# Seventeen gathered blocks instead of sixteen in the last block of a graph network, and a dense part of eight chunks of 512 nodes

## The chip, the cores and the metric

The kernel runs on one core of a Trainium2 chip. The metric is device time in microseconds: the median of three runs is 6218.43 us (6216.05 to 6231.69). The profiled execution of the same kernel took 7895.7 us, of which the trace covers 7893.8 us, so it is 1677 us longer than the median of the unprofiled runs. The trace does not say which parts of the kernel are shorter without the profiler; that gap matters for everything below.

## The reference: what is computed

A graph of N = 6250 nodes with 128 features each, and E = 106,250 directed edges sorted by destination, goes through four graph networks one after the other, each with a residual sum and a layer norm around it. The last one holds most of the work: three layers of three hops, nine hops in all, each of which sums weighted neighbour rows.

```
deg  = segment_sum(edge_attr, dst);  dinv = rsqrt(deg) where deg > 0, else 0
w    = dinv[src] * edge_attr * dinv[dst]
h    = node
for l in range(3):
    out, x = h @ W[l, 0], h
    for k in range(1, 4):
        x   = segment_sum(w[:, None] * x[src], dst)
        out = out + x @ W[l, k]
    y = h + out + bias[l]
    h = relu(layernorm(y) * gamma[l] + beta[l])
```

The first three networks do the same kind of sum with unweighted edges (a mean, and twice a symmetric normalisation).

## The kernel before

**Tiling.** The 6250 nodes are NW = 49 blocks of P = 128. The blocks of destination nodes are grouped into NC = 13 chunks, whose sizes in blocks are given by RUNS (line 64) and listed in SHAPE; START holds the first block of each. A chunk of four blocks is 512 columns, one of three is 384.

**Two ways to sum over neighbours.** A dense chunk uses an adjacency matrix in DRAM. For the unweighted sums this matrix is `counts` (one byte per cell) for all 13 chunks. For the nine weighted hops it is `weights` (four bytes per cell), made only for the first ND = 9 chunks, that is blocks 0 to 32. Both matrices are zeroed by transfers on SyncE's queue (`empty`) and then filled by GpSimd with scattered writes (`scatter`, line 571): 17 per block of edge rows. The other 16 blocks, GW = 33 to 48 with NG = 16, have no `weights`: in each hop GpSimd gathers their source rows, KG = 19 indirect transfers of 128 rows per block (line 1021, tile `rows`). ScalarE and VectorE multiply each gathered row by its edge weight and split it in two parts (lines 1055 and 1056, tile `both`), and TensorE adds the parts up with a one-hot matrix (line 1059, accumulator `gacc`). The one-hot matrices are made by VectorE (line 1037).

**A dense hop.** For each of the ND chunks TensorE multiplies the 49 blocks of the table of the hop before (`hop`) by 49 slices of `weights`, which arrive two at a time on SyncE's queue (tile `weighed`, line 453 issues, line 1091 multiplies, accumulator `acc`). A matmul of plain float32 shows as two MATMUL rows in the trace, so 441 products per hop are 882 rows.

**Order.** TensorE's order in the nine hops is fixed in the program. The class `Stream` (line 984) keeps a clock of its own, with a cost for each kind of work in its constants: DENSE for a product of 512 columns, GATHERED for a gathered product, SMALL and WIDE for the products at the end of a chunk, PACE for the time between two gathers on GpSimd, LAND for the time until gathered rows are usable. `take` puts a gathered product into TensorE's order when the planned landing time has come; `hop` puts the dense products there. The chip then runs this order as it stands: a gathered product that is not ready holds up every dense product behind it. GpSimd may run ahead by 26 gathers of the 30 row slots. The first gather of a hop waits until every block of the hop before is stored (`store`, line 893); `hop_end` does the closing work of a chunk (lines 925 to 981: transposes L419, small products L427 and L942).

**Ahead of the hops.** A first loop over the 13 chunks builds `counts` on GpSimd (`count_cells`, `cell` on VectorE) while TensorE computes the degrees (line 696) and the first sums (line 492). In the same loop `weights` is zeroed for chunks 0 to ND - 1, and from chunk ND - 1 on the second convolution's sums over the first KNOWN = START[ND] blocks are begun for chunks 0 to 7. Then `weights` is filled while TensorE works through the remaining unweighted sums, and three fetches for each gathered block (line 811) bring in its edges.

Of the kernel before, what the change touches and what calls it, by code (L numbers as in the profile page):

```python
# [33 lines left out]
F32 = mybir.dt.float32  # L34
# [4 lines left out]
I32 = mybir.dt.int32  # L39
# [8 lines left out]
P = 128  # L48
# [12 lines left out]
CW = 512  # L61
WPC = CW // P

RUNS = [(6, 4), (3, 3), (4, 4)]
SHAPE = [n for count, n in RUNS for _ in range(count)]
START = [sum(SHAPE[:c]) for c in range(len(SHAPE))]
NC = len(SHAPE)

KD = 17
# [2 lines left out]
assert KD * N == E and NB == NW  # L72
NEAR = 3

ND = 9
GW = range(START[ND], NW)
NG = len(GW)
PAIRS = [slice(w, min(w + 2, NW)) for w in GW[::2]]
# [6 lines left out]
SLOTS, LOADS, STEP, HOTS, GROUP = 30, 12, 2, 5, 4  # L85
# [17 lines left out]
def width(c):  # L103
    return len(windows_of(c)) * P
# [6 lines left out]
def near(i):  # L111
    begin = min(max(i - 1, 0), NW - NEAR)
    return range(begin, begin + NEAR)
# [6 lines left out]
def chunks_near(i):  # L120
    return sorted({chunk_of(near(i)[0]), chunk_of(near(i)[-1])})
# [53 lines left out]
def kernel(ctx: ExitStack, tc: tile.TileContext, a: dict, out: bass.AP):  # L175
# [13 lines left out]
    counts = dram.tile([BASE[NC], 1], U8, name="counts")  # L189
    weights = dram.tile([BASE[ND], 1], F32, name="weights")  # L190
    zeros = top.tile([P, 7 * CW // 16], F32, name="zeros")
# [162 lines left out]
    with tc.If(go == 1) as fork:  # L354
        usual_way(tc, a, out, dram, ident, part, first, recs, edges, counts, weights, fills, empty)
# [5 lines left out]
def usual_way(ctx, tc, a, out, dram, ident, part, first, recs, edges, counts, weights, fills, empty):  # L361
# [3 lines left out]
    work = ctx.enter_context(tc.tile_pool(name="work", bufs=2))  # L365
# [134 lines left out]
    def evicted(acc, cw, more=None):  # L500

        if more is not None:
            nc.vector.tensor_add(more[:, :cw], acc[:, :cw], more[:, :cw])
            return more
        t = sums_room()
        nc.scalar.copy(t[:, :cw], acc[:, :cw])  # L506
        return t
# [4 lines left out]
    celli = early.tile([P, NB, KD], I32, name="celli")  # L512
    dense = [i for i in range(NB) if chunks_near(i)[0] < ND]
    wval = early.tile([P, len(dense), KD], F32, name="wval")
# [14 lines left out]

    KNOWN, AHEAD = START[ND], 8  # L530
    halves = {c: dram.tile([P, width(c)], F32, name=f"half{c}") for c in range(1, NC)}
# [82 lines left out]
    with tc.tile_pool(name="counted", bufs=2) as counted, tc.tile_pool(name="cells", bufs=1) as cells, \  # L614
# [6 lines left out]
        def beside(x):  # L621

            return bass.AP(x.tensor, x.offset, [*x.ap[:-1], [1, KD], [1, J]])
# [6 lines left out]
        def cell(i, m):  # L630

            c0, c1 = chunks_near(i)[0], chunks_near(i)[-1]
            dst, source = m[:, F_DST:F_DST + KD], m[:, F_CELL:F_CELL + KD]
            mine = m[:, F_KEY + J:F_KEY + J + KD].unsqueeze(2).to_broadcast([P, KD, J])
            same = hots.tile([P, KD, J], BF16, name="same", bufs=1)
            before = hots.tile([P, KD, J], BF16, name="before", bufs=1)
            f1 = work.tile([P, KD], F32, name="f1")
            f2 = work.tile([P, KD], F32, name="f2")
            f3 = work.tile([P, KD], F32, name="f3")
            low = work.tile([P, KD], I32, name="low")  # L640
            dloc = cells.tile([P, KD], F32, name="dloc", bufs=12)
            lw = cells.tile([P, KD, 4], BF16, name="lw", bufs=12)
            degs[i] = dloc, lw
            w = m[:, F_W:F_W + KD]
            nc.vector.tensor_tensor(before[:], beside(m[:, F_KEY:F_KEY + KD]), mine, op=ALU.is_equal)
            nc.vector.tensor_reduce(f3[:], before[:], AX.X, ALU.max)
            nc.vector.tensor_tensor(same[:], beside(m[:, F_KEY + J + 1:F_KEY + J + 1 + KD]), mine, op=ALU.is_equal)
            nc.vector.tensor_reduce(f1[:], same[:], AX.X, ALU.add)
            nc.vector.tensor_scalar_add(cval[:, i, :], f1[:], 1.0)

            nc.vector.scalar_tensor_tensor(f2[:], source, float(width(c0)), dst, op0=ALU.mult, op1=ALU.add)
            nc.vector.tensor_sub(f2[:], f2[:], m[:, F_LOW:F_LOW + KD])
            nc.vector.tensor_scalar_add(f2[:], f2[:], float(BASE[c0] - START[c0] * P))
            if c0 < c1:
                turn, step = START[c1] * P, BASE[c1] - BASE[c0] - (START[c1] - START[c0]) * P
                f4 = work.tile([P, KD], F32, name="f4")
                if width(c0) == width(c1):
                    nc.vector.tensor_scalar(f4[:], dst, float(turn), float(step), op0=ALU.is_ge, op1=ALU.mult)
                else:
                    f5 = work.tile([P, KD], F32, name="f5")  # L660
                    nc.vector.tensor_scalar(f5[:], source, float(width(c1) - width(c0)), float(step),
                                            op0=ALU.mult, op1=ALU.add)
                    nc.vector.scalar_tensor_tensor(f4[:], dst, float(turn), f5[:], op0=ALU.is_ge, op1=ALU.mult)
                nc.vector.tensor_add(f2[:], f2[:], f4[:])
            if (i + 1) * P > ROWS:
                nc.vector.scalar_tensor_tensor(f3[:], dst, float(NOWHERE), f3[:], op0=ALU.is_ge, op1=ALU.add)
            nc.vector.scalar_tensor_tensor(celli[:, i, :], f3[:], FAR, f2[:], op0=ALU.mult, op1=ALU.max)
            nc.vector.tensor_copy(low[:], m[:, F_LOW:F_LOW + KD])
            nc.vector.tensor_tensor(celli[:, i, :], celli[:, i, :], low[:], op=ALU.bitwise_or)
            nc.vector.tensor_scalar_add(dloc[:], dst, -float(near(i)[0] * P))  # L670

            if i in dense:
                ew = hots.tile([P, KD, J], F32, name="ew", bufs=1)
                nc.vector.tensor_tensor(ew[:], same[:], beside(m[:, F_W + 1:F_W + 1 + KD]), op=ALU.mult)
                nc.vector.tensor_reduce(f1[:], ew[:], AX.X, ALU.add)
                nc.vector.tensor_add(wval[:, i, :], w, f1[:])
            nc.vector.tensor_copy(lw[:, :, 0], w)
            nc.vector.tensor_sub(f1[:], w, lw[:, :, 0])
            nc.vector.tensor_copy(lw[:, :, 1], f1[:])
            nc.vector.tensor_sub(lw[:, :, 2], f1[:], lw[:, :, 1])  # L680
            nc.vector.memset(lw[:, :, 3], 1.0)
# [49 lines left out]
        def count_cells(c):  # L731
            for i in fresh(c, counted_blocks):
                cell(i, fetched.pop(i))
                for _ in scatter(counts, U8, cval, i):
                    pass
                counted_blocks.add(i)
# [17 lines left out]
        for c in range(NC):  # L754
# [23 lines left out]
            nc.scalar.dma_start(bases[c][:], x[:])  # L778
            for e in range(2 * (c - ND + 1), 2 * (c - ND + 2)):
                if 0 <= e < AHEAD:  # L780
# [3 lines left out]
                    nc.scalar.dma_start(early_parts[e][:], evicted(acc, width(e), half)[:, :width(e)])  # L784
            if c < ND:
                empty(weights, F32, c, nc.sync)
# [196 lines left out]

    class Stream:

        DENSE, GATHERED, SMALL, WIDE, PACE, LAND, AHEAD = 0.86, 0.12, 0.29, 0.45, 1.26, 7.0, SLOTS - 4

        def __init__(self):
            self.clock = self.pool = 0.0
# [474 lines left out]
```

## Time and profile before

The profile's own time is divided here by the first matmul of line 1091 in each hop.

| What | us |
|---|---|
| Median of the runs | 6218.4 |
| Profiled execution, its span | 7895.7, 7893.8 |
| From the start to the first hop | 3227.2 |
| Nine hops, sum | 4666.6 |
| A hop, six without and three with the layer's end | 505 to 521, 534 |
| TensorE busy in the hops | 3938.6 |
| GpSimd busy in the hops | 2704.2 |
| One gather on GpSimd, median and mean busy time | 0.944, 0.988 |

Engine names in the profile: PE is TensorE, PEld its weight loads, DVE VectorE, ACT ScalarE, POOL GpSimd, SP SyncE; a small q behind a name is the engine's issuing sequencer. A row of the timeline gives start, length, engine, line, operation, output and inputs, how many instructions are merged, and in brackets the idle time before it and what ended it. The length of a matmul overlaps with the next one, so durations of matmuls are read from start to start.

### The profile page before, as it was taken

What the parts mean: (1) busy time and instruction counts of PE and PEld (TensorE: products, weight loads), DVE (VectorE), ACT (ScalarE), POOL (GpSimd) and SP (SyncE); (2) the same over time, 40 slices, a digit from 0 to 9 for tenths busy, and PEclk for the clock granted to TensorE, in tenths of its full rate; (3) what the DMA queues carried; (4) which work ended last, traced back from release to release, by engine and by line L of the source; (5) the groups of instructions that cost most, each with busy time, mean ns of one, the idle gap of its engine ahead of it and who ended that gap; (6) DMA issues with size and microseconds to landing.
All of it is one profiled execution on the core that took longest, in us unless ns stands there. A gap on an engine that the chain in (4) does not pass through costs nothing. (4 is left out here: it accounts for less than half of the span.)

```text
span 7893.8 us, 73018 instructions
## 1 busy us (share of the span) xinstructions
PE 5805.9 (74%) x20184; PEld 3479.6 (44%) x20184; DVE 2979.8 (38%) x8549; ACT 1995.5 (25%) x4437; POOL 4220.2 (53%) x4207
## 2 busy tenths in 40 slices
PE   1354544339668499789798888897888978878887
PEld 0132333117556388445344454453444534434444
DVE  5344323112555256333232452332324423333355
ACT  1122223115344244222121221221212212122122
POOL 5655455640556501364664654646646556466464
PEclk8666767559879799899898998998989989989898
DMA  7444543013343245577677776776767767777776
GB/s 229 125 148 120 168 136 103 13 30 97 106 116 103 56 130 151 194 264 269 229 263 238 256 244 238 276 266 225 260 240 254 248 234 273 244 248 257 253 279 214
DMA packets 720126, 1539.01 MB, mean 195 GB/s; under 512 B 136004, under 2 KB 349144, under 8 KB 719448
## 3 DMA queue, kind: packets, MB, share of 16 engines
q1 hardware_dynamic: 536448, 1292.14, 48.4%
q0 software_dynamic: 134496, 181.90, 7.9%
q10 hardware_dynamic: 48760, 60.19, 2.2%
q8 instruction: 161, 2.64, 0.1%
q14 instruction: 261, 2.14, 0.1%
HBM read 1337.46 MB, written 196.32 MB: 194 GB/s over the span
## 5 line engine op out<-in xcount | busy, mean ns | idle before, releaser
L1091 PE MATMUL acc<-weighed,hop 128*128 128x512 f32 (+1 forms) x7938 | 3681.6, 581 | 336.0 <-issue 326.9
L1021 POOL DMA_INDIRECT rows<-stored,gsrc x2736 | 2704.2, 988 | 2028.4 <-issue 866.7
L1091 PEld LDWEIGHTS acc<-weighed,hop 128*128 128x128 f32 x7938 | 1374.7, 198 | 1423.8 <-issue 1174.2
L1059 PE MATMUL gacc<-both,oh 128*128 128x256 f32 x2736 | 1733.2, 641 | 99.7 <-issue 98.0
L1055 ACT ACTIVATE both<-rows,gwgt 128x128 fp32r<-128x128 f32 x2736 | 879.2, 390 | 2895.0 <-issue 1115.7
L1056 DVE SCALAR_TENSOR_TENSOR both<-rows,gwgt,both 128x128 fp32r<-128x128 f32 x2736 | 831.6, 348 | 1525.2 <-ACT both L1055 718.8
L492 PE MATMUL acc<-wides,t 128*128 128x512 f32 (+1 forms) x3105 | 969.7, 422 | 559.6 <-ACT wides L481 316.3
L571 POOL DMA_INDIRECT counts<-cval,celli x833 | 856.6, 1028 | 591.4 <-issue 248.5
L571 POOL DMA_INDIRECT weights<-wval,celli x578 | 607.3, 1051 | 656.0 <-PE acc L492 479.9
L492 PEld LDWEIGHTS acc<-wides,t 128*128 128x128 f32 x3105 | 617.3, 208 | 752.9 <-ACT wides L481 396.6
L1059 PEld LDWEIGHTS gacc<-both,oh 128*128 128x128 f32 x2736 | 541.0, 198 | 731.1 <-issue 582.5
L1037 DVE TENSOR_TENSOR oh<-iota,gdst 128x640 fp32r<-128x640 f16 x576 | 453.9, 788 | 1030.1 <-remote 356.8
L481 ACT CAST wides<-slots 128x1024 fp32r<-128x1024 uint8 (+3 forms) x687 | 572.2, 863 | 932.2 <-remote 480.1
L492 PE MATMUL acc<-widev,t 128*128 128x512 f32 (+1 forms) x2034 | 594.6, 402 | 62.2 <-DVE widev L481 45.6
L695 DVE TENSOR_SCALAR oh<-iota,dloc 128x384 bf16<-128x384 f16 x833 | 225.8, 324 | 893.5 <-remote 428.6
L492 PEld LDWEIGHTS acc<-widev,t 128*128 128x128 f32 x2034 | 386.3, 198 | 146.0 <-DVE widev L481 66.3
L696 PE MATMUL pd<-oh,lw 128*4 128x384 bf16 x833 | 211.6, 370 | 253.6 <-issue 160.7
L481 ACT CAST wides<-cols 128x1024 fp32r<-128x1024 uint8 (+1 forms) x364 | 286.9, 797 | 402.0 <-PE acc L492 166.4
L481 DVE CAST widev<-cols 128x1024 fp32r<-128x1024 uint8 (+1 forms) x364 | 243.0, 669 | 343.8 <-PE acc L492 208.3
L696 PEld LDWEIGHTS <-lw 128*4 128x4 bf16 x833 | 66.3, 88 | 336.4 <-issue 290.4
L481 DVE CAST widev<-slots 128x1024 fp32r<-128x1024 uint8 (+2 forms) x237 | 155.1, 665 | 121.3 <-remote 53.8
L492 PE MATMUL half<-wides,t 128*128 128x512 f32 (+1 forms) x594 | 186.8, 395 | 0.0
(232 smaller groups left out, 2813.0 us busy)
## 6 DMA issues: line engine op xcount, KB each, us to landing
weighed<-weights SPq DMA_DIRECT2D x1296, 512.0 KB
weighed<-weights SPq DMA_DIRECT2D x648, 384.0 KB
slots<-counts SPq DMA_DIRECT2D x173, 448.0 KB
weights<-zeros SPq DMA_DIRECT2D x6, 12544.0 KB
cols<-counts SPq DMA_DIRECT2D x140, 448.0 KB
rows<-stored,gsrc POOLq DMA_INDIRECT x2736
counts<-zeros SPq DMA_DIRECT2D x10, 3136.0 KB
weights<-zeros SPq DMA_DIRECT2D x3, 9408.0 KB
```

What stands on the lines that cost most here:

```text
L481: copy(wide[:, :n * cw], t[:, r * cw:(r + n) * cw])
L492: product = nc.tensor.matmul(into[:, :cw], lhs, cols, start=s == begin and i == 0, stop=s == end - 1 and i == len(lhss) - 1).ins
L571: ins = nc.gpsimd.indirect_dma_start(out=mat[:], out_offset=bass.IndirectOffsetOnAxis(ap=celli[:, i, k:k + 1], axis=0), in_=vals[:, i, k:k ...
L695: nc.vector.tensor_scalar(oh[:], iota[:], dloc[:, k:k + 1], None, op0=ALU.is_equal)
L696: nc.tensor.matmul(acc[:], lw[:, k, :], oh[:], start=k == 0, stop=k == KD - 1)
L1021: nc.gpsimd.indirect_dma_start(out=fetched_rows[:, self.slot(self.asked), :], out_offset=None, in_=stored[self.h % 2][:], in_offset=bass.I ...
L1037: nc.vector.tensor_tensor(oh[:, :m, :], iota[:, :P].unsqueeze(1).to_broadcast([P, m, P]), gdst[:, i, ks].unsqueeze(2).to_broadcast([P, m, ...
L1055: nc.scalar.activation(both[:, :D], x, AF.Copy, scale=w)
L1056: nc.vector.scalar_tensor_tensor(both[:, D:], x, w, both[:, :D].bitcast(F32), op0=ALU.mult, op1=ALU.subtract)
L1059: nc.tensor.matmul(self.acc[:, j * 2 * D:(j + 1) * 2 * D], self.oh[:, k % HOTS, :], both, start=k == 0, stop=k == KG - 1)
L1091: nc.tensor.matmul(acc[:, :cw], tables[h][:, s, :], t[:, s % STEP * cw:(s % STEP + 1) * cw], start=s == 0, stop=s == NW - 1)
```

## The change

Three constants and four allocations change. RUNS gives ten chunks of four blocks and then three of three, in place of six, three of three, and four. With ND = 8 the weighted dense part is chunks 0 to 7, all of 512 columns (blocks 0 to 32 become 0 to 31), and GW becomes blocks 32 to 48, so NG is 17: eight pairs and a single block at the end. The small tiles f1 to f5 and `low` of `cell` move from the pool `work`, which lives for the whole kernel, to the pool `cells`, which ends with the first loop, with two buffers as before. PACE in the plan goes from 1.26 to 1.2; LAND and the other constants stay.

```diff
-RUNS = [(6, 4), (3, 3), (4, 4)]
+RUNS = [(8, 4), (2, 4), (3, 3)]
...
-ND = 9
+ND = 8
...
-            f1 = work.tile([P, KD], F32, name="f1")
+            f1 = cells.tile([P, KD], F32, name="f1", bufs=2)
...
-            low = work.tile([P, KD], I32, name="low")
+            low = cells.tile([P, KD], I32, name="low", bufs=2)
...
-                f4 = work.tile([P, KD], F32, name="f4")
+                f4 = cells.tile([P, KD], F32, name="f4", bufs=2)
...
-        DENSE, GATHERED, SMALL, WIDE, PACE, LAND, AHEAD = 0.86, 0.12, 0.29, 0.45, 1.26, 7.0, SLOTS - 4
+        DENSE, GATHERED, SMALL, WIDE, PACE, LAND, AHEAD = 0.86, 0.12, 0.29, 0.45, 1.2, 7.0, SLOTS - 4
```

What follows from the constants, without further edits: a hop has 392 dense products of 512 columns where it had 294 of 512 and 147 of 384; it has 323 gathers where it had 304, so 2907 in all for 2736; 200 loads of `weights` per hop for 225; 561 scattered writes into `weights` for 578; 51 fetches of gathered edges for 48; eight zero fills of `weights` for nine; and the early sums of the second convolution begin one chunk earlier and cover 32 blocks for 33, the 33rd being left to the later loop.

More of the change, by code (lines that the diff above doesn't have):

```diff
@@ L636, in cell @@
             before = hots.tile([P, KD, J], BF16, name="before", bufs=1)
-            f1 = work.tile([P, KD], F32, name="f1")
-            f2 = work.tile([P, KD], F32, name="f2")
-            f3 = work.tile([P, KD], F32, name="f3")
-            low = work.tile([P, KD], I32, name="low")
+            f1 = cells.tile([P, KD], F32, name="f1", bufs=2)
+            f2 = cells.tile([P, KD], F32, name="f2", bufs=2)
+            f3 = cells.tile([P, KD], F32, name="f3", bufs=2)
+            low = cells.tile([P, KD], I32, name="low", bufs=2)
             dloc = cells.tile([P, KD], F32, name="dloc", bufs=12)
@@ L659, in cell @@
                 else:
-                    f5 = work.tile([P, KD], F32, name="f5")
+                    f5 = cells.tile([P, KD], F32, name="f5", bufs=2)
                     nc.vector.tensor_scalar(f5[:], source, float(width(c1) - width(c0)), float(step),
```

## The prediction

> **What bounds the kernel now.** I read the page first: PE is busy 74% of the span, POOL 53%, and the slices show two regimes. Up to 3227 us the engines are all half idle; from there on nine hops repeat, 4666.6 us or 59% of the span. The change acts on the hops, so I cut them out by the first matmul of line 1091 and asked for the windows. One typical hop:
>
> ```profile
> core 0: us, PE busy (x) PEld busy (x) DVE busy (x) ACT busy (x) POOL busy (x), PEclk, DMA share, GB/s
> ...
> 5297.80:5805.10 507.30, 433.97 (x1303) 230.51 (x1302) 167.96 (x448) 106.30 (x330) 300.19 (x304) 0.91 0.73 255
> ```
>
> PE is busy 434 of 507 us, POOL 300, DMA 73%: PE is nearest to its limit, but not at it. The busy figure overstates PE, because lengths of matmuls overlap, so I took start-to-start times from PE's timeline where nothing waits:
>
> ```profile
> 5549.81 1.02 PE L1091 MATMUL acc<-weighed,hop 128*128 128x512 f32 x2
> 5550.27 0.68 PE L1059 MATMUL gacc<-both,oh 128*128 128x256 f32 x1
> 5550.79 1.88 PE L1091 MATMUL acc<-weighed,hop 128*128 128x512 f32 x4
> 5552.10 0.68 PE L1059 MATMUL gacc<-both,oh 128*128 128x256 f32 x1
> 5552.62 1.02 PE L1091 MATMUL acc<-weighed,hop 128*128 128x512 f32 x2
> 5553.08 0.68 PE L1059 MATMUL gacc<-both,oh 128*128 128x256 f32 x1
> 5553.59 1.02 PE L1091 MATMUL acc<-weighed,hop 128*128 128x512 f32 x2
> ```
>
> One product (two rows) and one gathered product take 0.98 us, two products and one gathered 1.83: a product of 512 columns costs 0.855 us, a gathered one 0.12. In the same way 5798.55 to 5799.96 gives 0.645 for 384 columns, 5568.72 to 5570.44 gives 1.72 for the closing of a chunk of four (0.43 a block), and a gathered pair's transposes and products cost 0.22 + 0.44 = 0.66. PE's own work in this hop is then 294 x 0.855 + 147 x 0.645 + 304 x 0.12 + 33 x 0.43 + 8 x 0.66 = 402 us. **105 us of the hop are lost on PE.** Some 45 us of them lie in one stretch near the start of each hop, in which every PE instruction, weight loads too, comes 0.7 us or a multiple after the one before:
>
> ```profile
> 5335.01 0.86 PE L1091 MATMUL acc<-weighed,hop 128*128 128x512 f32 x1 [2.20 <-issue]
> 5337.81 1.01 PE L1091 MATMUL acc<-weighed,hop 128*128 128x512 f32 x1 [1.94 <-issue]
> 5339.91 1.01 PE L1091 MATMUL acc<-weighed,hop 128*128 128x512 f32 x1 [1.09 <-issue]
> ```
>
> "Issue" says that no semaphore explains it. The other engine to look at is POOL. Its waits in the hop, and its last gather with the first of the next hop:
>
> ```profile
> POOL rows L1021 <- issue: 134.3, 236, 58.1
> POOL rows L1021 <- DVE both L1056: 61.0, 32, 8.7
> ```
>
> ```profile
> 5757.74 1.06 POOL L1021 DMA_INDIRECT rows<-stored,gsrc  x1 [0.30 <-issue]
> 5816.06 0.94 POOL L1021 DMA_INDIRECT rows<-stored,gsrc  x1 [57.26 <-DMA weighed<-weights]
> 5817.31 0.94 POOL L1021 DMA_INDIRECT rows<-stored,gsrc  x1 [0.30 <-issue]
> ```
>
> POOL waits 61 us for row slots, which DVE frees at PE's pace, and 57 us between hops. The row of the last gather (5757.74) is multiplied only at 5800.96, 43 us later. So in this execution PE holds up POOL, and not POOL PE.
>
> **The change, part by part.**
>
> *Dense products.* 392 x 0.855 = 335.2 us replace 346.2: -11.0 us a hop on PE. *Gathered products:* 19 more, +2.3. *Closing work:* 32 dense blocks for 33, -0.4; one gathered block more, +0.3. **Sum: -8.8 us a hop**, from 402 to 393. The three hops that end a layer are some 27 us longer, from the layer norm, before and after alike. In the ninth hop the last gathered block, not the dense part, leads to the last output, and there are more gathers, so I count eight hops: -70 us.
>
> *19 more gathers on POOL.* Two gathers start 1.249 us apart (5816.06 to 5829.80 holds eleven steps): +23.7 us a hop. The shortest hop that POOL allows is 303 x 1.249 = 378.4, plus 4.7 from a gather to ACT's first use (5310.42 to 5315.10), about 1 to PE, and 15.1 from the last gathered product to the next hop's first gather (5800.96 to 5816.06): 399 us before, 423 after. Against 507 - 9 = 498 this is covered with 75 us to spare, by PE. If that cover is gone, POOL decides; that is the rival below.
>
> *ACT and DVE.* 19 x 0.39 and 19 x 0.349 + 4 x 0.82 for one-hot matrices: +7 and +10 us on engines busy 106 and 168 of 507. Nothing.
>
> *PACE.* It only changes PE's fixed order. At 1.2 against a measured 1.249, the order asks for the last row 323 x 0.049 = 16 us early, less the margin between LAND (7.0) and the 5.7 above. Behind a waiting gathered product stand all dense products, and behind these the stores that the next hop's gathers wait for. In the profile rows lie 43 us ready, so it costs nothing there; without this lead PE waits, as part of POOL's 423.
>
> *Transfers.* Here a rule speaks against the change. The Trainium skill, DMA: Bandwidth & Descriptors, section Bandwidth, gives 0.95 us of transfer time for 64 KB and wants transfers of 1 MiB. A gather is 64 KB; the change takes 512 KB loads away for such. The rows:
>
> ```profile
> q1 hardware_dynamic: 32339, 105.76, 58.1%
> q0 software_dynamic: 9728, 19.94, 12.6%
> ```
>
> By the row a gather takes 507.3 x 0.126 / 304 = 0.21 us of the 16 engines, so +4.0 us; the loads fall by 6272 columns x 512 B = 3.2 MB at 2.8 us per MB, -9.0: together -5. By the rule, were a gather to occupy the engines alone, my estimate is +18 - 9 = +9. The trace does not agree with it here, since gathers overlap with loads; I take the row. With 73% busy neither is on the path.
>
> *Ahead of the hops.* 17 scattered writes fewer are 17 x 1.276 = 22 us of POOL in a stretch of 810 us in which it is busy 452; three fetches more lie beside PE's last unweighted sums; the setup's comparisons grow from 800 to 850 columns, under 1 us. The early sums start a chunk earlier, in a loop of 1610 us with PE busy 650, and the last chunk of that loop has 384 columns for 512, which may shorten its 260 us tail by some 10. On the other side the wider chunks 6 to 8 ask for their cells earlier, and POOL waits over 30 us per chunk for DVE there. I take 0, with -30 to +20. The tiles f1 to f5 keep two buffers: no new wait.
>
> **Likeliest: faster by 70 us, 6148 us** (profiled 7896 - 70 = 7826). The profiled execution is 1677 us longer than the runs, and the trace can't say where. If everything shrinks alike, by 6218 / 7896 = 0.79, POOL's 423 becomes 333 while the hop is 400: PE stays the bound. The own range is 6120 to 6195: 79 us for nine hops and some gain ahead of them, down to a third where POOL takes part of it back.
>
> **Rival 1: POOL becomes the bound, slower.** Its place is the end of each hop, its price 423 against PE's 402 before. It decides if, off the profile, the gathers keep their 1.249 us while PE's lost time goes: those 0.7 us steps look like nothing that the program asks for. With a loss L per hop on PE, before is 402 + L and after is 423, so it is slower from L under 21, by 9 x (21 - L); at L = 26 almost half of the gain is gone. For L = 8: +117 us, **6335 us**. For it: POOL's step is the same in every hop, whatever the load. Against it: in all nine hops POOL waits for PE, and 75 us of slack must go first. An L of 0 would give 6406, which I leave out, since a hop that meets every landing exactly is unlikely.
>
> **Rival 2: no change**, within 0.3% (19 us, about what a measurement of this kernel tells from none): PE and POOL meet near L = 21, **6218 us**. The crossing is narrow.
>
> **Chances.** Likeliest 0.57, rival 1 0.35, rival 2 0.08; so faster 0.57, same 0.08, slower 0.35. The range runs from 6120 to rival 1 at L = 6, 6350; about 0.15 stays outside, most of it above.
>
> **What would show it.** Right: in the profile after, hops 8 to 9 us shorter, POOL still waiting for row slots (tens of us per hop) and idle 40 us or more between hops, DMA share unchanged. Wrong by rival 1: PE waiting before L1059 for ACT or DVE, POOL's steps at 1.25 without waits for DVE, last gather and last gathered product only 6 us apart. The two need not agree: a profile with shorter hops beside slower runs would say that the profiler's lost time on PE was the cover. Wrong otherwise: the first hop's start moved by more than 30 us.

## The result, and the profile after

The changed kernel takes 6329.25 us (6312.93 to 6332.02, four runs) against 6225.06 for the kernel before in the same session: ratio 1.016, interval 1.0148 to 1.0173. It is slower by 104 us, where 70 us less were forecast.

The profile shown before, and the runs e9 to e18 below (on other chips than e1 to e8), come from executions in which every kernel, the one before too, took some 27% longer for a reason that is not shown, so from those only ratios to the kernel before, run beside them, are used. A second profile of the kernel before (e1) has a span of 6216.3 us and agrees with the runs; the profile after has 6329.7. These two are compared. The windows of one hop within a layer, cut at the first dense product as in the prediction and with the columns given there, first the kernel before (e1):

```profile
4044.20:4470.60 426.40, 408.89 (x1303) 223.01 (x1302) 178.18 (x448) 125.75 (x330) 299.61 (x304) 0.98 0.90 304
```

and the changed kernel:

```profile
4067.90:4510.20 442.30, 410.90 (x1217) 212.77 (x1216) 186.07 (x465) 131.96 (x347) 319.88 (x323) 0.96 0.85 288
```

At run time a hop of the kernel before is 426 us, not 507, and has 426 - 401 = 25 us lost on PE instead of 105. The changed kernel needs 16 us more, although PE has 8 to 9 us less of its own to do. The waits of that hop in the changed kernel (engine, line and releaser; us in total, times, longest):

```profile
DVE both L1056 <- ACT both L1055: 239.4, 239, 10.5
ACT both L1055 <- DMA rows<-stored,gsrc: 236.9, 228, 6.8
...
POOL rows L1021 <- issue: 42.4, 139, 0.3
...
PE pp L942 <- ACT agg L506: 27.8, 8, 6.8
POOL rows L1021 <- DMA weighed<-weights: 25.5, 1, 25.5
POOL rows L1021 <- DVE both L1056: 25.0, 82, 0.3
```

POOL does not wait for row slots: the longest of its 82 waits behind DVE is the 0.3 us that lies between any two gathers, where in the first profile it reached 8.7. Its only real pause is the 25.5 us at the turn of the hop, from its last gather to the next hop's first. Rows are taken as they land: ACT waits for them 228 times. Both hold at run time for the kernel before as well, so neither is what the change brought; its hop in e1:

```profile
ACT both L1055 <- DMA rows<-stored,gsrc: 232.1, 224, 8.9
...
POOL rows L1021 <- DVE both L1056: 24.4, 80, 0.3
...
PE pp L942 <- ACT agg L506: 11.6, 4, 6.7
```

What grew is PE's wait, and it is not at a gathered product but at line 942, the closing of a dense chunk. The groups from 2300 to 6160 us, which is all of the hops but the end of the ninth (busy and mean of one, then PE's idle time before them), the kernel before:

```profile
L942 PE MATMUL pp<-wk,agg 128*128 128x256 f32 x396 | 117.6, 447 | 70.3 <-ACT agg L506 70.2
L427 PE MATMUL pp<-wk,xT 128*128 128x128 f32 x484 | 73.5, 282 | 15.8 <-ACT xT L421 15.8
L419 PE MATMUL pp<-ident,h 128*128 128x128 f32 x140 | 27.8, 281 | 27.1 <-DVE h L926 27.1
```

and the changed one:

```profile
L1059 PE MATMUL gacc<-both,oh 128*128 128x256 f32 x2780 | 1836.2, 669 | 9.9 <-DVE oh L1037 9.7 <-DVE both L1056 0.2
L942 PE MATMUL pp<-wk,agg 128*128 128x256 f32 x384 | 133.6, 508 | 129.0 <-ACT agg L506 129.0
L427 PE MATMUL pp<-wk,xT 128*128 128x128 f32 x490 | 75.4, 282 | 15.6 <-ACT xT L421 15.6
L419 PE MATMUL pp<-ident,h 128*128 128x128 f32 x146 | 32.2, 300 | 68.8 <-DVE h L926 68.7
```

The two closings (942 for dense, 419 for gathered chunks) wait 100 us more in this stretch; the gathered products wait 9.9 us. One such closing in the changed kernel, PE's timeline first:

```profile
4182.03 1.02 PE L1091 MATMUL acc<-weighed,hop 128*128 128x512 f32 x2
4182.49 0.68 PE L1059 MATMUL gacc<-both,oh 128*128 128x256 f32 x1
...
4183.99 1.02 PE L1091 MATMUL acc<-weighed,hop 128*128 128x512 f32 x2
4184.44 0.68 PE L1059 MATMUL gacc<-both,oh 128*128 128x256 f32 x1
4189.66 3.78 PE L942 MATMUL pp<-wk,agg 128*128 128x256 f32 x8 [4.53 <-ACT agg L506]
```

and ACT in the same microseconds:

```profile
4185.74 0.40 ACT L1055 ACTIVATE both<-rows,gwgt 128x128 fp32r<-128x128 f32 x1 [0.98 <-DMA rows<-stored,gsrc]
4187.25 0.40 ACT L1055 ACTIVATE both<-rows,gwgt 128x128 fp32r<-128x128 f32 x1 [1.11 <-DMA rows<-stored,gsrc]
4188.73 0.40 ACT L1055 ACTIVATE both<-rows,gwgt 128x128 fp32r<-128x128 f32 x1 [1.09 <-DMA rows<-stored,gsrc]
4189.04 0.56 ACT L506 COPY agg<-acc 128x512 f32<-128x512 f32 x1
```

The chunk's last products start by 4184.4. The copy of its sums (line 506) needs 0.56 us of ACT, but three scalings stand ahead of it in ACT's queue, and each waits for a row that is still on its way. PE, which has the closing next in its fixed order, stands still until the third row has landed. Line 419, too, waits for what ACT and DVE make (lines 925 and 926); an example of it is not shown.

Each such wait costs more than its length. During it or right after, the clock that is granted to TensorE falls to half (0.50, the column behind the engines):

```profile
4187.60:4194.40 6.80, 4.74 (x11) 3.51 (x11) 4.25 (x12) 2.61 (x8) 5.22 (x6) 0.50 0.38 139
```

The closing at 4189.66 lies in this stretch and takes 3.78 us for its eight products; the one at 4155.29, before which PE did not wait, takes 1.89 at full clock. In the fourth to the sixth hop of the changed kernel there are 17 such stretches of 3.4 to 10.2 us, 102 us in all, and each begins during or right after a pause of PE of 2.0 us or more; in e1 there are 9, 48 us in all.

The transfers of this hop, by queue (packets, MB, share of the 16 engines):

```profile
q1 hardware_dynamic: 28776, 102.70, 66.0%
q0 software_dynamic: 10267, 21.05, 17.1%
```

The loads fell by 3.4 MB from the hop of e1 (106.06), with the DMA share at 0.85 for 0.90. They are not what grew. The first hop starts at 2298.0 us for 2305.0, so nothing was lost ahead of the hops.

### The profile page after: what moved, and what is told of

Same layout as the page of the kernel before. It is cut to its first block, busy times and chain, and to the rows that moved or that the text cites. A ratio compares the mean times of both kernels' runs of the same rounds, so it can differ in the third digit from the quotient of the medians.

```text
span 6329.7 us, 72113 instructions
## 1 busy us (share of the span) xinstructions
PE 5398.9 (85%) x19482; PEld 3218.7 (51%) x19482; DVE 3154.8 (50%) x8758; ACT 2219.7 (35%) x4612; POOL 4450.7 (70%) x4364
## 5 line engine op out<-in xcount | busy, mean ns | idle before, releaser
L1021 POOL DMA_INDIRECT rows<-stored,gsrc x2907 | 2888.2, 994 | 1224.6 <-issue 394.3
L1091 PE MATMUL acc<-weighed,hop 128*128 128x512 f32 x7056 | 3432.5, 600 | 6.0 <-DMA weighed<-weights 6.0
L1055 ACT ACTIVATE both<-rows,gwgt 128x128 fp32r<-128x128 f32 x2907 | 1122.1, 399 | 2542.0 <-DMA rows<-stored,gsrc 2104.2
L1056 DVE SCALAR_TENSOR_TENSOR both<-rows,gwgt,both 128x128 fp32r<-128x128 f32 x2907 | 994.4, 351 | 1955.9 <-ACT both L1055 1946.0
L1059 PE MATMUL gacc<-both,oh 128*128 128x256 f32 x2907 | 1908.7, 667 | 23.5 <-DVE both L1056 12.4
L1091 PEld LDWEIGHTS acc<-weighed,hop 128*128 128x128 f32 x7056 | 1164.7, 193 | 955.5 <-issue 886.7
L492 PE MATMUL acc<-wides,t 128*128 128x512 f32 (+1 forms) x3077 | 876.0, 394 | 277.9 <-ACT wides L481 277.4
L492 PEld LDWEIGHTS acc<-wides,t 128*128 128x128 f32 x3077 | 570.0, 191 | 410.9 <-ACT wides L481 246.1
L942 PE MATMUL pp<-wk,agg 128*128 128x256 f32 x384 | 133.6, 508 | 129.0 <-ACT agg L506 129.0
L942 PEld LDWEIGHTS pp<-wk,agg 128*128 128x128 f32 x384 | 93.3, 254 | 167.5 <-ACT agg L506 148.7
```

The lines of the kernel that those rows point to most:

```text
L492: product = nc.tensor.matmul(into[:, :cw], lhs, cols, start=s == begin and i == 0, stop=s == end - 1 and i == len(lhss) - 1).ins
L942: nc.tensor.matmul(pm[:, j * 2 * D:(j + 1) * 2 * D], agg[:, (b + j) * P:(b + j + 1) * P], wt["wk"][:, i::12 - i, :], start=True, stop=True)
L1021: nc.gpsimd.indirect_dma_start(out=fetched_rows[:, self.slot(self.asked), :], out_offset=None, in_=stored[self.h % 2][:], in_offset=bass.I ...
L1055: nc.scalar.activation(both[:, :D], x, AF.Copy, scale=w)
L1056: nc.vector.scalar_tensor_tensor(both[:, D:], x, w, both[:, :D].bitcast(F32), op0=ALU.mult, op1=ALU.subtract)
L1059: nc.tensor.matmul(self.acc[:, j * 2 * D:(j + 1) * 2 * D], self.oh[:, k % HOTS, :], both, start=k == 0, stop=k == KG - 1)
```

## The experiments

Two theories stood at the start. **A: POOL's chain** of 323 gathers decides (the prediction's rival 1). **B: PACE.** At 1.20 PE's fixed order asks for the rows earlier than POOL delivers them. In the second profile of the kernel before, the gathers of the fourth hop stand 1.29 us apart in the mean (391.9 us from the first to the last of 304; the median is 1.249), and POOL never waits for a slot there, so this is its own rate.

**e1**, the kernel before once more, gave the profile above.

> The kernel before, unchanged, profiled a second time. If the 1677 us that the first profile had above the runs were that one execution's own, the span is now within 1% of 6225, the first hop starts within 30 us of the 2298 of the kernel after, and a hop without a layer's end takes 405 to 430 us. If profiling always slows this kernel, the span is above 7500 again. What is read from it for both theories: where POOL's chain (last gather to next hop's first) and PE's waits before L1059 stand before the change. Theory A (POOL's chain became the bound): before, PE waits under 10 us a hop for gathered rows. Theory B (the plan's PACE of 1.2 asks for rows too early): the same.

It took 6218.12 us (one run).

**e2, the change without its PACE; e3, PACE alone.**

```diff
-        ... PACE, LAND, AHEAD = 0.86, 0.12, 0.29, 0.45, 1.2, 7.0, SLOTS - 4
+        ... PACE, LAND, AHEAD = 0.86, 0.12, 0.29, 0.45, 1.26, 7.0, SLOTS - 4
```

(e2 in the changed kernel; e3 the reverse in the kernel before.)

> The kernel after with PACE back at 1.26; 17 gathered blocks stay. Theory A, the gathers' chain of 323 steps decides: the order of the products matters little, 6290 to 6345. Theory B, the order is what costs: 6230 or less.

> The kernel before with PACE 1.2 and its 16 gathered blocks. Theory A: POOL has 19 gathers less, so at most 30 us slower than before, 6225 to 6255. Theory B: the order alone brings the loss, +80 us or more, above 6305.

e2: 6229.81 us, ratio 1.0011 (1.0004 to 1.0017). e3: 6375.74 us, ratio 1.0247 (1.0229 to 1.0264). Both as B said. The seventeenth block alone costs and brings almost nothing; PACE 1.20 alone makes the kernel before slower than the whole change does.

**e4, the changed kernel without the gathers of the seventeenth block.** Its products take rows that lie in the slots already, so part of the sums is left out; the order stays.

```diff
+                if i < NG - 1:
-                nc.gpsimd.indirect_dma_start(
+                    nc.gpsimd.indirect_dma_start(
```

> The kernel after without the 19 gathers of the 17th block: its products, scalings and one-hot matrices stay and read whatever rows the slots hold, so the last block's sums are not computed from its edges; the planned order is unchanged. Theory A: each hop is shorter by up to 19 x 1.30 = 25 us until PE's own 393 us and its closing decide, 6110 to 6190. Theory B: all rows before the 17th block are asked for as early as before, so PE waits as before: 6290 to 6345.

6294.68 us, ratio 1.0126 (1.0106 to 1.0146). 19 gathers fewer per hop buy 35 us of the 104 by the medians, about 21 by the ratios. With that, A does not explain the loss.

**e5, PACE upward in the kernel before.** If B is a drift, in which each row costs the difference between the true step and PACE, the kernel before still pays for 1.29 - 1.26.

```diff
-        ... PACE, LAND, AHEAD = 0.86, 0.12, 0.29, 0.45, 1.26, 7.0, SLOTS - 4
+        ... PACE, LAND, AHEAD = 0.86, 0.12, 0.29, 0.45, 1.3, 7.0, SLOTS - 4
```

> The kernel before, PACE 1.26 made 1.30, nothing else. The gathers of its second profile (the one that ran at the time of the runs) stand 1.29 us apart in the mean. Theory B1, drift: PE's written order takes the rows at PACE, POOL delivers them at 1.29, so each of the 304 rows of a hop costs PE max(0, 1.29 - PACE) wherever it happens to wait; 1.26 leaves 304 x 0.03 = 9 us a hop, 1.30 leaves none: 8 x 9 = 72 us less, and with the ends of the layers a little more, 6110 to 6180. Theory B2, a cliff: only a PACE under the pipeline's median step of 1.249 asks too early, and 1.26 is already free of it: 6210 to 6240. Theory A, POOL's chain alone decides (here 304 gathers as before): 6210 to 6240.

6165.6 us, ratio 0.9898 (0.9873 to 0.9923), as drift expected. The sizes agree in one layer of three hops (the fourth to the sixth, cut at their first dense products). PE's own work is counted from the rows with the lengths of the prediction; "lost" is the rest, and the last column is the time for which the granted clock stood at half:

| Kernel | three hops, us | PE's own work | lost | at half clock |
|---|---|---|---|---|
| before (e1), PACE 1.26 | 1302.7 | 1212 | 91 | 48 |
| e3, before with 1.20 | 1361.0 | 1212 | 149 | 96 |
| e5, before with 1.30 | 1277.7 | 1212 | 66 | 41 |
| changed, 1.20 | 1350.2 | 1186 | 164 | 102 |
| e2, changed with 1.26 | 1298.0 | 1187 | 111 | 65 |

From 1.26 to 1.20 a hop grows by 58.3 / 3 = 19.4 us in the kernel before, where 304 x 0.06 = 18.2, and by 52.2 / 3 = 17.4 in the changed one, where 323 x 0.06 = 19.4. From 1.26 to 1.30 it shrinks by 8.3, where 304 x (1.29 - 1.26) = 9.1. About a quarter of what is lost is work at half clock: with PE idle for 10 of the 48 us in the first row and for 25 of the 102 in the fourth, half of the rest is 19 of 91 and 39 of 164 us (an estimate). The half-clock time moves with PACE in one and the same kernel (48, 96 and 41 us for 1.26, 1.20 and 1.30), so it is part of PACE's price and not a second cause.

**e6 and e7: are the closings the cause, or only where PE meets the lateness?** The order leaves 2.4 us of plan time between a dense chunk's end and its closing, and 4.0 for a gathered one.

```diff
-            yield 0.0, 4.0
+            yield 0.0, 8.0
...
-            yield 0.0, 2.4
+            yield 0.0, 8.0 if ws.stop < of(ND - 1)[1].stop else 2.4
```

> The changed kernel (PACE 1.2), with the closing products of a dense chunk 8.0 instead of 2.4 us of plan time behind its end (the last chunk of a hop keeps 2.4), those of a gathered chunk 8.0 instead of 4.0. In the changed kernel's profile PE waits 129 us for the evicted sums at the closings (line 942) and 69 us at line 419, almost nothing at the gathered products. Theory C, the closings: evictions stand in ACT's queue behind scalings whose rows have not landed, and the time is lost because the closings come too soon behind them; moved back, the waits at the two lines fall under 80 us together and the time falls to 6215 to 6265. Theory B1, drift: the lateness of the rows (323 x 0.09 = 29 us a hop by its end) has to be paid somewhere, the waits only move to the gathered products or to the later closings: 6305 to 6345.

> The kernel before (PACE 1.26), with the closings moved back as in e6. Its second profile has 70 us of waits at line 942 and 37 us at line 419. Theory C, the closings: most of these 107 us go, 6120 to 6180. Theory B1, drift: 6205 to 6240, the waits only move.

e6: 6358.62 us, ratio 1.0196 (1.0178 to 1.0213), slower than the changed kernel and a little above the range that drift expected. e7: 6229.52 us, 0.9988 (0.9981 to 0.9995), as drift expected. The groups of e6, same window:

```profile
L942 PE MATMUL pp<-wk,agg 128*128 128x256 f32 x384 | 97.4, 399 | 24.9 <-ACT agg L506 24.9
L427 PE MATMUL pp<-wk,xT 128*128 128x128 f32 x490 | 90.5, 318 | 160.8 <-ACT xT L421 160.7
L419 PE MATMUL pp<-ident,h 128*128 128x128 f32 x144 | 29.2, 280 | 36.8 <-DVE h L926 36.7
```

The wait at line 942 went from 129 to 25 us, and that at line 427, the next product of PE that needs a copy from ACT, from 16 to 161. In the three hops PE lost 166 us for 164. So the lateness is paid at whatever product next depends on ACT's queue; moving that product moves the wait.

**e8, e2 without the gathers of the seventeenth block** (the edit of e4, with PACE 1.26; part of the sums is left out).

> The changed kernel with PACE 1.26 (as e2) and without the 19 gathers of the seventeenth block (its products take rows that lie there already, so this leaves out part of the sums); the order is otherwise e2's. In e2 a hop's dense chunks end 60 to 75 us before its last gathered product, and the next hop's first gather follows the last one by 8 to 11 us. Theory D, with a PACE near the true step POOL's 323 gathers are what e2's hop waits for: 19 x 1.29 = 24.5 us less a hop until the dense chunks' own end decides, 6040 to 6130. Theory PE: e2's hop is bound by PE's order and not by the number of gathers: 6200 to 6235.

6195.34 us, ratio 0.9934 (0.9918 to 0.9951). This is between the two: the 19 gathers cost e2 some 0.8%, against the 9 x 24.5 = 220 us (3.5%) that they would cost if POOL alone set the hop. Theory D is too strong and theory PE too weak. The pause of POOL at the turn of the hop shows why they meet in e2. Kernel before (e1), last gather and next hop's first (the bracket is the idle time before it):

```profile
4446.83 0.94 POOL L1021 DMA_INDIRECT rows<-stored,gsrc  x1 [0.31 <-issue]
4481.72 0.94 POOL L1021 DMA_INDIRECT rows<-stored,gsrc  x1 [33.94 <-DMA weighed<-weights]
```

and e2:

```profile
4482.80 0.94 POOL L1021 DMA_INDIRECT rows<-stored,gsrc  x1 [0.30 <-DVE both L1056]
4494.13 0.94 POOL L1021 DMA_INDIRECT rows<-stored,gsrc  x1 [10.38 <-issue]
```

34 us of pause became 10: POOL's longer chain fills the time in which the kernel before waited for its last dense chunk, and from first gather to first gather both hops take 426 us (4055.8 to 4481.7 and 4067.6 to 4494.1).

**e9 and e15, PACE 1.30 in the changed kernel.** These and the runs that follow are the 27% longer ones. In them the rows lie ready, as in the first profile. ACT's waits for a landing row over the whole program, first in the changed kernel, then in e17, the same kernel in a longer execution:

```profile
ACT both L1055 <- DMA rows<-stored,gsrc: 2104.2, 2031, 9.1
```

```profile
ACT both L1055 <- DMA rows<-stored,gsrc: 173.9, 78, 21.6
```

ACT scales a row 36 us after its gather starts (mean of e17), where it is 5 us at run time. So a longer execution cannot show what late rows cost, only what another order costs.

> The changed kernel with PACE 1.30. Drift alone would give, from e2's 6230, another 323 x 0.03 = 9.7 us a hop, 78 us in all: 6140 to 6180. POOL's rate: with 323 gathers a hop cannot be shorter than 323 x 1.29 + 9 = 426 us (e2 has 421 to 451), whatever the order; nothing is won behind e2: 6215 to 6260.

> The changed kernel with PACE 1.30 (e9 again, for the same reason). Drift alone: 9.7 us a hop less than e2, ratio to before 0.986 to 0.993. POOL's rate: 323 x 1.29 + 9 = 426 us a hop whatever the order, 0.998 to 1.006.

Ratios 0.9973 (0.9958 to 0.9988) and 0.9982 (0.9962 to 1.0003): nothing like the 0.986 to 0.993 of drift alone. The second lies where POOL's rate expected it, the first just below; but POOL also waited for row slots here, so that its rate is the reason is not shown.

**e10 and e16, PACE 1.34 in the kernel before.**

> The kernel before with PACE 1.34, above POOL's true mean step of 1.29. If only a PACE below the true step costs: 6150 to 6185, as e5. If the rows' places in the order decide on both sides: the last takes of a hop stand 304 x 0.04 = 12 us later than in e5, and the hop's turn moves with them, up to 97 us: 6200 to 6265.

> The kernel before with PACE 1.34 (e10 again, for the same reason). If only a PACE below the true step of 1.29 costs: 0.986 to 0.994, as e5 (0.990). If places in the order that are too late cost as well: the last takes of a hop stand 12 us later than in e5, ratio 0.996 to 1.006.

0.9866 (0.9828 to 0.9904) and 0.9879 (0.9827 to 0.9931). A larger PACE helps there too; whether 1.34 is too large at run time is not shown, since the gathers stood 1.5 us apart in these runs. The expectations of e13 to e18 take these 1.5 us for POOL's own step. In part they are not: POOL waits for row slots (292 waits, 570.6 us in e17), as in the first profile.

**e11, PACE 1.30 and the later closings in the kernel before.**

> The kernel before with PACE 1.30 and the closings of e6 and e7 (8.0 us behind the end). In e5 the waits of PE at lines 942, 419 and 427 are still 46, 15 and 34 us. If, with the drift gone, these are lost because the closings stand too close behind the end, half of them or more go: 6090 to 6140. If they only mirror rows that are late elsewhere: 6150 to 6185.

0.9924 (0.9895 to 0.9953). Without e5 under the same conditions this settles nothing.

**e12, e13, e18 and e14: all takes 15 us later, at an unchanged rate.** This was to tell lateness from density: an offset leaves the rate of the takes as it is.

```diff
-        ... PACE, LAND, AHEAD = 0.86, 0.12, 0.29, 0.45, 1.2, 7.0, SLOTS - 4
+        ... PACE, LAND, AHEAD = 0.86, 0.12, 0.29, 0.45, 1.2, 22.0, SLOTS - 4
```

> The changed kernel, PACE 1.2, with LAND 22 instead of 7: every take stands 15 us later in the order, its rate is unchanged. Drift: the rows' lateness in the order, which grows to 323 x 0.09 = 29 us by a hop's end, is 15 us smaller all along, and the first half of a hop has none: half to all of the 99 us between the changed kernel and e2 come back, 6225 to 6285. Rate of the takes: PACE 1.2 asks ACT and DVE for scalings too densely, an offset changes nothing: 6315 to 6345.

> The changed kernel, PACE 1.2, with LAND 22 instead of 7: every take stands 15 us later in the order, its rate is unchanged (e12 again, to be compared where the gathers stand 1.29 us apart as in e1 to e8). Drift: the rows' lateness in the order, 323 x 0.09 = 29 us at a hop's end, is 15 us smaller all along: half to all of the 1.5% between the changed kernel and e2 comes back, ratio to before 1.000 to 1.009. Density of the takes: an offset changes nothing, 1.013 to 1.019.

> The kernel before with PACE 1.20 (e3, 1.0247) and LAND 22. Drift: the lateness of 304 x 0.09 = 27 us at a hop's end falls to 12 us and is gone in the first half of a hop: half to all of e3's loss comes back, ratio 1.000 to 1.013. Density: 1.021 to 1.028.

> The changed kernel once more, beside e18. Where the gathers stand 1.29 us apart: 1.014 to 1.018, as measured. Where they stand 1.5 us apart (as in e9 to e16) the order with PACE 1.20 is late by 323 x 0.3 = 97 us a hop and the 19 more gathers cost 19 x 1.5 = 28 us each hop: drift expects more than there, 1.018 to 1.035, density no more than 1.016.

> As e13 (LAND 22 in the changed kernel), to be set beside e17. Drift: 0.5% to 1.5% below e17. Density: within 0.3% of e17.

e12 1.0099 (1.0061 to 1.0136) and e13 1.0119 (1.0072 to 1.0167) had no changed kernel beside them; e13 lies between the two expectations. e17, the changed kernel: 1.0225 (1.0205 to 1.0244). e18, beside it: 1.0135 (1.0087 to 1.0183). The offset gives back 0.9%, within what drift expected, and the intervals do not overlap. e14: 1.0006 (0.9977 to 1.0034), where e3 without the offset was 1.0247 at run time. So density alone does not fit e18: an order that takes later costs less. But these runs do not show that late rows are the reason, since the rows lay ready in them. What is late there is ACT's scaling; of its waits, 750.8 us in e17 are for PE, and 876.6 us are "issue", for which the profile shows no reason. For the same reason the larger loss of the changed kernel there (1.0225 for 1.016) is not explained. That the rows' lateness is what costs at run time rests on the sizes of e2, e3 and e5 and on ACT's waits, not on these runs; the offset was not tried where rows are taken as they land.

## Why the prediction was wrong, point by point

**The step that failed: PACE, "it costs nothing there".** The prediction computed the lateness (323 x 0.049 = 16 us a hop, with the median step) and then set it to nothing, because rows lay 43 us ready in the profile. Priced with the mean step it is 323 x 0.09 = 29 us, of which the old PACE already paid 9.7. At run time no row lies ready: POOL has no wait for a slot and ACT waits for rows 228 times in a hop. e2 and e3 show the price: 99 us in the changed kernel (6329 for 6230), 153 in the one before (6376 for 6223). That is 99 of the 174 us between forecast and result; the other 75 are the gain that did not arrive (below). Nor was the order free where rows did lie ready: in the longer executions the changed kernel stands at 1.0225 with PACE 1.20 (e17) and at 0.9973 and 0.9982 with 1.30 (e9, e15). The prediction put ACT at "nothing" by its busy time, and busy it is for only 132 of 442 us; the path runs through the order of its queue. In the changed kernel the price is smaller than 52 us a layer would give over three layers, because the last hop ends with its last gathered rows in either order, so that a lead of the dense part is lost there: from the seventh hop's first dense product to the last gathered product the changed kernel takes 1339.1 us and e2 1344.5. The prediction's fallback, that PE would then wait "as part of POOL's 423", was wrong too: in e3, with POOL's chain unchanged, a hop is 442 to 448 us long.

**"105 us of the hop are lost on PE"** held for that execution only. 25 us are lost at run time, so the 75 us of cover before POOL decides were not there. The prediction saw that the profile was 1677 us longer than the runs and spread this evenly over everything; it put its forecast on a cover that the runs did not have to have. Its own column of the clock (0.91) was a sign: PE stood at half clock for 96 us of that hop, 48 of them from 5335.2 to 5383.0, the stretch of the 0.7 us steps, and for 14 us of the hop in e1. Half clock alone does not make such steps; what does is not shown. Nor is it shown that PE held up POOL there: ACT and DVE free the slots, and of ACT's waits before a scaling 1115.7 us are "issue", 465.2 for PE.

**Dense and gathered products, -8.8 us a hop: right.** PE's own work falls by 25 to 26 us in three hops. But in e2's total none of it arrives. The first eight hops of e2 take 3414 us for 3464 in e1, so 50 us are won; the ninth takes 519 for 447, because its dense part is done 89 us before its last gathered product (3 us in e1). From the last gathered product of the first hop to that of the ninth both need nearly the same, 3476 us in e2 and 3467 in e1. The lead of the dense part ends in a wait for the gathered rows, and counting eight hops did not allow for that. e8 says that the 19 gathers cost part of it (0.8%); the rest is not taken apart.

**POOL: 399 and 423 us.** The step of 1.249 is a median; with the mean of 1.29 the chain is longer, 392 us from the first gather to the last for 304 and about 416 for 323. The forecast's 4.7 + 1 + 15.1 = 20.8 us from the last gather to the next hop's first were not the gathers' own: in four of e2's eight turns it is 9 to 11 us. The two errors nearly cancel there: 416 + 10 = 426, where the forecast had 423.

**Transfers and the stretch ahead of the hops: right.** -3.4 MB of loads a hop and a first hop 7 us earlier.

**Rival 1** named almost the time, 6335, for the wrong cause. With L = 25, as measured, its formula gives 9 x (21 - 25) = -36, not slower. Two of its signs failed as well: PE hardly waits before line 1059, and the last product comes 18 us after the last gather starts, not 6. The third, steps of 1.25 us without waits for slots, was seen, but it holds for the kernel before as well (e1). That the number was near is luck. **Rival 2** is what the change without PACE does (e2).

## What to carry to other kernels

A static order is a promise on a rate, so fix its rate from the mean step of the slowest feeder, not from its median, and from an execution as long as the runs. An order that asks too early by d per item cost about d times the items here (e2, e3, e5), but the profile books the wait at another place: at the next instruction whose input comes through the same in-order queue, here a 0.6 us copy behind scalings that wait for rows. Before a change that gives work to the engine with the most slack, check that the slack exists in an execution of the runs' length. Of the kernels measured at run time, the one before with PACE 1.30 and sixteen blocks is the fastest, 6165.6 us.

## What the runs showed of the hardware

- In the changed kernel and e1 to e8, gathers of 128 rows of 512 B issue 1.249 to 1.252 us apart in the median and 1.28 to 1.33 in the mean of a hop; a few take 1.5 to 4.9 us. Over a hop the tail adds 9 to 26 us.
- In the longer executions (e9 to e18) the gathers stand 1.47 to 1.56 us apart in the mean with a median of still 1.25, with gaps up to 23 us, in part waits for row slots. The median hides this entirely.
- At full clock PE's products cost the same in both: a product of 512 columns and a gathered one take 0.98 us from start to start here (4182.03 to 4183.99 holds two such pairs) as in the prediction. It is the time between them that differs, and the clock behind it.
- During or right after a wait of PE the granted clock stood at half for 3.4 to 10.2 us, and eight closing products took 3.78 us for 1.89. In the fourth to the sixth hop no such stretch came without a pause of at least 2.0 us (the changed kernel and e1); not every such pause brought one (2.3 us at 4243.9).
